# Two-layer cross-attention on one core: two row copies placed apart, a doubled result written by one add, and one projection step put later

## The chip, the cores and the metric

The kernel runs on one core of a Trainium2 chip. The metric is the time of one execution in microseconds of device time. Engines are named as in the profile: PE (TensorE, its weight loads apart as PEld), DVE (VectorE), ACT (ScalarE), POOL (GpSimd) and SP (SyncE, which issues most DMAs).

## The reference

Two attention layers follow each other on 16 images of 256 tokens with 320 channels, against a context of 256 rows with 512 channels. The first 77 context rows are text in layer 1 and the others image tokens; in layer 2 the last four are image tokens. The first layer, cut to what matters here:

```
text, ip = ctx[:, :77], ctx[:, 77:]
text_out = softmax(q_h @ k_h.T * scale) @ v_h              # 20 heads of 16
scores   = q_h @ ip_k_h.T * scale                          # per head
sem      = softmax(q @ k_text.T * scale) @ text @ ip.T * scale   # all heads alike
ip_probs = softmax(scores + 0.5 * sem) * spatial_mask
out      = (text_out + ip_probs @ ip_v_h) @ Wout + bout + x
```

Layer 2 has the same frame, with a semantic term of its own for each head (normalised rows of the text average against normalised image rows) that is added to the scores of the four image tokens.

## The kernel before

**Tiling.** The 20 heads of an image are worked in NG = 5 groups of four. One group of one image is a *slot*: 80 slots of layer 1 (`slot0(k)`, image k // 5, group k % 5), then 80 of layer 2 (`slot1(k)`). Beside a slot's own work run *tasks*: generators for the projections of keys, queries and values, the semantic term and the output projection (`close0`, `close1`), each with a list of due times counted in slots. `fill(now)` steps all tasks that are due, by the smallest due time.

**Layer 1.** For each group a stacked query tile Q (`qs`) and key tile K (`ks`) are built. Their first 77 rows carry the semantic term: the transposed text probabilities `tph`, copied to all four heads of Q (the T copy, L621, 77x1024), and the semantic key rows M, copied into the image columns of K (the M copy, L623, 77x716). Both are ACT's. Below these rows come the group's own rows, loaded by two DMAs ("K" and "Q"). Four such stacks exist; for the first four groups of an image the rows must be copied, and with LEAD = 4 it was done for group k + 4 at the end of slot k. `score0` multiplies K and Q (PE L650) and DVE takes the maxima of text and image columns (L651, L652). `maxima0` turns them on PE (L658), casts them on ACT (mt, L660) and puts them into Q by a DMA from ACT's queue (L661). `turned0` multiplies with keys on the rows (PE L673), takes exponentials on ACT (L676) and multiplies them by the semantic exponentials on POOL (L679), for two halves t of the keys. `attend0` multiplies by the values (PE L709). `settle0` transposes (DVE L720), divides (L723 to L726) and adds the text and the image part into `hsn` on POOL (L727). `hsn` has room for six groups; the fifth is written twice, by the add and then by a copy (L729).

**Output projection.** `close0` and `close1` go through `finish`: for three pairs of groups a 128x256 piece is made in a PSUM bank (in layer 1 by a DVE transpose of `hsn`, L953), and split into a rounded and a remainder part (ACT L744, DVE L746; for the third pair DVE L748). Then `project` multiplies by the output weights in three steps (PE L523, tile names `ho` and `wF`), and DVE adds bias and residual (L763).

**Layer 2.** `maxima1` (PE L801), `attend1` (PE L836, L838), `both1` (PE L784, L789) and `norm1` (PE L823, DVE L826, L828) play the same parts; L491 is the last of the DVE instructions that build the tile `gm` of the next image from an X bank.

**What sets the order.** Only PE's order is the program's own. For ACT, DVE, POOL and SP a scheduler orders the instructions. `queued(inst, *behind)` puts an instruction behind others of its engine without a wait: behind those named, or behind the last one marked by `anchor` on that engine (in layer 1 the DVE maxima L652, the exponentials and the POOL multiplies). PSUM is parted into three X banks, in which all projections, transposes and semantic products take turns, two T banks, one P bank and one of two banks' size for the scores.

Of the kernel before, what the change touches and what calls it, by code (L numbers as in the profile page):

```python
# [16 lines left out]
B = 16  # L17
S = 256
# [5 lines left out]
T0 = 77  # L24
# [13 lines left out]
NS = B * NG  # L38
LEAD = 4


def RAMP(t):
    return t if t < -5 or t > 3 else (t + 5) * 0.375
# [5 lines left out]
def xattn2(  # L49
# [27 lines left out]
    nc = tc.nc  # L77
    f = lambda ap: ap.bitcast(F32)
    mm = nc.tensor.matmul

    def dma(out, in_):
        nc.sync.dma_start(*(f(ap) if ap.dtype == FR else ap for ap in (out, in_)))  # L82
# [6 lines left out]
    def bank(tag="X"):  # L89
        return ps.tile([128, 512], F32, tag=tag, name=tag, bufs=BANKS[tag])  # L90
# [449 lines left out]
    def stack_rows(d):  # L540
        return d.rearrange("r (d h) t -> (r d) h t", h=HP)
# [64 lines left out]

    QK, P, W, R = {}, {}, {}, {}

    def stacks0(k, parts="KQTM"):
        b, g = divmod(k, NG)  # L610
        Q, K = QK[k] = qs[k % SIZES["NR"]], ks[k % SIZES["NR"]]
        hs = slice(4 * g, 4 * g + 4)
        for part in parts:
            if part == "K":
                dma(K[T0 : T0 + XROW], stack_rows(kd[0][b // 2][:, :, b % 2])[:, hs])
            elif part == "Q":
                dma(Q[T0 : T0 + XROW], stack_rows(get("q0", b)[1])[:, hs])
            elif g < SIZES["NR"]:
                tph, mh = get("s0", b)[1::2] if part == "T" else (None, get("m0t", b))
                if part == "T":  # L620
                    nc.scalar.copy(Q[:T0], f(tph[:, 0:1]).to_broadcast([T0, 4, S]))  # L621
                else:
                    nc.scalar.copy(K[:T0, :, T0:], f(mh[:, 0:1, T0:]).to_broadcast([T0, 4, S - T0]))  # L623


    def stacks1(k):
        b, g = divmod(k - NS, NG)
        n = 2 * SIZES["NR"]
        i = ((NS - SIZES["NR"]) % SIZES["NR"]) * 2 + (k - NS) % n
        Q, K = QK[k] = [x[i // 2 % SIZES["NR"]][:, 2 * (i % 2) : 2 * (i % 2) + 2] for x in (qs, ks)]  # L630
        get("k1", b)
        qd = get("o1", b)[0]
        for u in range(2):
            rows = slice(64 * u, 64 * u + XROW)
            hs = slice(4 * g + u, 4 * g + u + 3, 2)
            if k - NS < n:
                dma(K[64 * u + XROW : 64 * u + KS1], w1["ind"])
            dma(K[rows], stack_rows(kd[1][b][:, :, 0])[:, hs])
            dma(Q[rows], stack_rows(qd)[:, hs])
# [14 lines left out]
    def maxima0(k, queue=nc.scalar):  # L654
        Q, mn = QK[k][0], maxes[k]
        mp = bank()
        for t in range(2):
            mm(mp[:8, t * 128 : (t + 1) * 128], mn[:, t].rearrange("p a h -> p (a h)"), ident_r, start=True, stop=True)  # L658
        mt = buf("mt", [8, S], FR)
        nc.scalar.copy(mt, mp[:8, :S])  # L660
        issues[k] = queue.dma_start(f(Q[KS0 - 2 : KS0]), f(mt))  # L661

    def turned0(k, t):
# [17 lines left out]
    def attend0(k):  # L681
        b, g = divmod(k, NG)
        v, pv = get("v0", b), bank("P")
        for vt in range(3):
            values0(k, pv, v, vt)
        settle0(b, g, pv)

    def slot0(k):
        if k > 0:
            yield lambda: maxima(k + 1)  # L690
        yield lambda: ahead(k + 2, 0)
        yield lambda: turned0(k, 0)
        yield 0.2
        if k == 2:
            yield lambda: stacks(k + LEAD - 1)
        if k > 0:
            yield lambda: attend0(k - 1)
        yield lambda: ahead(k + 2, 1)
        yield lambda: turned0(k, 1)
        if k != 1:  # L700
            yield lambda: stacks(k + LEAD)
        yield 0.6
        yield 1.0

# [12 lines left out]
    def settle0(b, g, pv):  # L717
        hn = hsn
        nt = buf("nt", [128, 2, 8, 32], bufs=2)
        nc.vector.transpose(nt.rearrange("p a f c -> p (a f c)"), pv)  # L720

        rz = pv[:, :16].rearrange("p (a f) -> p a f", a=2)
        nc.vector.reciprocal(rz, nt[:, :, :, 16])  # L723
        nc.vector.tensor_mul(rz[:, 1], rz[:, 1], mk)
        tmp = buf("tmp", [128, 2, 8, 16], bufs=2)
        nc.vector.tensor_mul(tmp, nt[:, :, :, 0:16], rz.unsqueeze(3).to_broadcast([128, 2, 8, 16]))  # L726
        nc.gpsimd.tensor_add(hn[:, g // 2, :, g % 2], tmp[:, 0], tmp[:, 1])  # L727
        if g == NG - 1:
            nc.gpsimd.tensor_copy(hn[:, 2, :, 1], hn[:, 2, :, 0])  # L729

    def gather(b):

# [207 lines left out]
    def close1(b):  # L940
        hT, (pT, bd) = results["gathered", b], get("i1", b)

        def rows(p, hp):
            mm(hp, bd[:, p * 128 : (p + 1) * 128], pT, start=True, stop=True)  # L944
            nc.vector.tensor_add(hp, hT[:, p], hp)

        y = yield from finish(1, b, load(x1d[b], "xc"), rows)
        dma(out_d[b].rearrange("(k p) t -> p k t", p=128), y)

    def close0(b):  # L950

        def rows(p, hp):
            nc.vector.transpose(hp, hsn[:, p].rearrange("p f r d -> p (f r d)"))  # L953

        x1 = yield from finish(0, b, resid0.pop() if b == 0 else load(xT_d[b], "xc"), rows)
        dma(x1d[b].rearrange("(k p) t -> p k t", p=128), x1)
# [21 lines left out]
    def task(key, times, make, *needs):  # L978
        tasks[key] = [times, 0, make, needs, len(tasks)]
# [14 lines left out]
    def get(*key):  # L994
        while key not in results:
            step(key)
        return results[key]
# [20 lines left out]
    def shifted(n, *times):  # L1018

        return [RAMP(n + t) for t in times]  # L1020
# [10 lines left out]
    for c in range(B // 2):  # L1031
        n, k = 10 * c, [("k0", c)] if c else []
        task(("k0", c), FIRST["k0"] if c == 1 else shifted(n, -14.4, -13.3, -13, -12.4, -12, -10.8, -10.4, -9.8, -9.4, -8.8, -8.4), (lambda c=c: keys0(c)) if c else first_keys,
             *([("w4", 0)] if c > 1 else []))
        task(("q0", 2 * c), shifted(n, -11.8, -11, -10, -9, -8), lambda b=2 * c: queries0(b))
        task(("q0", 2 * c + 1), shifted(n, -4.4, -4, -3, -2.8, -2), lambda b=2 * c + 1: queries0(b))
        task(("m0t", 2 * c), shifted(n, -7.4), lambda b=2 * c: tokens0(b), *k)
        task(("m0t", 2 * c + 1), shifted(n, -4.8), lambda b=2 * c + 1: tokens0(b), *k)
        task(("v0", 2 * c), shifted(n, -7, -5.4, -5), lambda b=2 * c: values0_(b), *k)
        task(("v0", 2 * c + 1), shifted(n, -4, -3.8, -3.4), lambda b=2 * c + 1: values0_(b), *k)  # L1040
        for b, t in ((2 * c, (-7.4, -6.4, -6, -5.4, -5, -4.4, -3.4)), (2 * c + 1, (-2.4, -1.4, -1, -0.8, -0.4, 0, 1.2))):
            task(("s0", b), FIRST["s0"] if b == 1 else shifted(n, *t), lambda b=b: semantic0(b), ("q0", b), ("m0t", b))
            task(("c0", b), shifted(5 * b, *((5.6, 6, 6.2, 7.2, 7.6, 8.2) if b % 2 == 0 else (5.6, 6, 6.2, 7.2, 8.2, 9.2) if b < B - 1 else (6.33, 6.67, 7, 7.67, 8, 8.67))), lambda b=b: close0(b), ("w4", 0))
    for b in range(B):
        n = NS + 5 * b
        task(("k1", b), shifted(n, -7, -6.67, -6.33, -5.67, -5, -4.67), lambda b=b: keys1(b), ("w2",), *([("t1", b - 1)] if b else []), *([("w4", 1)] if b > 2 else []))
        task(("t1", b), shifted(n, -3.67, -3, -2.67, -2.33), lambda b=b: tokens1(b), ("k1", b), ("w3", b % 2))
        task(("o1", b), shifted(n, -7.67, -7, -6.67, -5.33, -4.33, -4), lambda b=b: open1(b), ("w7",), ("c0", b), *([("o1", b - 1)] if b else []))
        task(("i1", b), shifted(n, 6.67, 6.67, 6.67, 6.67, 7.33, 7.33, 7.67, 7.67, 8, 8.33), lambda b=b: image_softmax(b, NG - 1 if b == B - 1 else 0), ("gathered", b), ("taken", B + b - 1), *([("i1a",)] if b == B - 1 else []))
        task(("c1", b), shifted(n + (1.67 if b > B - 3 else 0), 8.67, 9, 9.33, 10, 11.67, 13), lambda b=b: close1(b), ("i1", b), ("w4", 1))  # L1050
    task(("i1a",), [2 * NS + 0.1], lambda: image_softmax(B - 1, 0, NG - 1), ("i1", B - 2))
    spread = lambda t, d, n: [t + d * i for i in range(n)]
    thirds = lambda n, t: [t + i // 3 + (0.2, 0.6, 1.0)[i % 3] for i in range(n)]
# [6 lines left out]
    task(("w4", 0), [2.6, 2.8, 3, 3.2], lambda: weights4(0), ("k0", 1))  # L1060
    task(("w4", 1), spread(NS + 4, 0.33, 4), lambda: weights4(1), ("c0", B - 1))

    def stacks(k):
        if 0 <= k < 2 * NS:
            (stacks0 if k < NS else stacks1)(k)

    def ahead(k, t):
        if k < NS:
            score0(k, t)
        else:  # L1070
            both1(k - 2, t)

    def maxima(k):
        if k < 2 * NS:
            (maxima0 if k < NS else maxima1)(k)
# [131 lines left out]
```

## Time and profile before

| | us |
|---|---|
| three runs | 1600.88, 1594.26, 1597.96 (median 1597.96) |
| the profiled execution: its own time | 1597.92 |
| its span in the trace | 1596.1 |
| mean granted TensorE clock | 0.983 |
| a pair of images in layer 1, from one of the waits at L650 to the next (126.50, 208.72, 290.94 us) | 82.22 |
| an image in layer 2, from one wait at L523 to the next (867.77, 921.31 us) | 53.54 |

A row of a group gives line, engine, operation, tiles and shapes, then its busy time, the mean of one in ns, and the idle time of the engine ahead of it with what ended it. A row of the timeline gives start, length, engine and instruction (several in a row of one kind as xN), and in brackets the idle time ahead of it and its releaser. Layer 1 runs to about 700 us, layer 2 behind it.

### The profile page before, as it was taken

Reading aid. Unit: us, or ns where it says so; the run is one execution under the profiler, and the core shown is the slowest. Engines: PE = TensorE matmul, PEld = TensorE weight load, DVE = VectorE, ACT = ScalarE, POOL = GpSimd, SP = SyncE. Lnnn points to the kernel's source line nnn. Section 1 sums busy time; section 2 is a strip of 40 time slices with the busy share of each in tenths; the row PEclk is TensorE's granted clock in tenths of the full one; section 3 lists DMA queues with packets and bytes.
Section 4 is the critical chain, followed back from the end, with each engine's and each line's share of the span. In section 5 each row is a group of like instructions: output and inputs, shape, how many; then the busy total and the mean of one; then the engine's idle time right before and its main releaser. Section 6 shows DMA issues by size and latency. Waiting matters only on the chain.

```text
span 1596.1 us, 35022 instructions
## 1 busy us (share of the span) xinstructions
PE 1493.3 (94%) x12666; PEld 1213.0 (76%) x12666; DVE 1211.1 (76%) x2468; ACT 944.8 (59%) x2071; POOL 1162.0 (73%) x1194
## 2 busy tenths in 40 slices
PE   7798989898989999799999999999999999999997
PEld 6677878787878888577777777777777777777765
DVE  5366667676767687887888888888888888888796
ACT  5556666666666676655565555555555555555563
POOL 3458787877777777787777777777777777767775
PEclk9999999999999999899999999999999999999999
DMA  6755556564646374555424333433344243423301
GB/s 217 183 151 158 156 153 169 143 173 119 187 124 189 113 208 117 151 180 176 130 85 130 122 121 97 137 122 112 106 128 131 87 131 112 144 82 106 111 26 55
DMA packets 206425, 213.09 MB, mean 134 GB/s; under 512 B 29162, under 2 KB 190156, under 8 KB 206252
## 3 DMA queue, kind: packets, MB, share of 16 engines
q1 hardware_dynamic: 204512, 209.56, 44.9%
q8 instruction: 100, 1.64, 0.4%
q10 hardware_dynamic: 1740, 1.30, 0.3%
q14 instruction: 73, 0.60, 0.1%
HBM read 121.21 MB, written 88.18 MB: 131 GB/s over the span
## 4 chain that ended last, share of the span: by engine, by line
PE 80%; DVE 6%; ACT 4%; POOL 4%; issue 3%; DMA 2%; SPq 1%; ACTq 0%; POOLq 0%; DVEq 0%
PE X L205 20%; PE X L823 16%; PE X L523 11%; PE P L709 6%; PE S L650 5%; PE P L836 4%; PE T L673 4%; PE T L784 4%; PE P L838 3%; PE S L789 2%; POOL P L679 2%; PE X L572 1%; PE X L944 1%; DVE mn L790 1%; SPq L82 1%
## 5 line engine op out<-in xcount | busy, mean ns | idle before, releaser
L679 POOL TENSOR_TENSOR P<-P,rs 128x512 f32<-128x512 f32 x320 | 410.1, 1303 | 140.3 <-ACT P L676 139.4
L814 POOL TENSOR_TENSOR wt<-P,ctb 128x512 f32<-128x512 f32 x320 | 417.1, 1320 | 117.0 <-ACT ctb L813 116.6
L823 PE MATMUL X<-ctb,gm 128*128 128x512 f32 x1120 | 330.1, 413 | 2.0 <-DVE wt L826 1.8
L676 ACT ACTIVATE P<-T 128x512 f32<-128x512 f32 x320 | 174.7, 593 | 147.8 <-PE T L673 137.7
L795 ACT ACTIVATE P<-T 128x512 f32<-128x512 f32 x320 | 174.0, 597 | 127.1 <-PE T L784 126.3
L813 ACT ACTIVATE ctb<-P 128x512 fp32r<-128x512 f32 x320 | 195.2, 632 | 60.8 <-PE X L823 59.8
L823 PEld LDWEIGHTS X<-ctb,gm 128*128 128x128 f32 x1120 | 189.5, 188 | 48.6 <-DVE wt L826 2.8
L790 DVE TENSOR_REDUCE mn<-S 128x4 fp32r<-128x1008 f32 x160 | 192.0, 1200 | 0.2 <-PE S L789 0.2
L826 DVE TENSOR_TENSOR wt<-X,wt 128x512 f32<-128x512 f32 x240 | 161.8, 679 | 10.7 <-PE X L823 9.7
L652 DVE TENSOR_REDUCE mn<-S 128x4 fp32r<-128x716 f32 x160 | 142.6, 891 | 0.0
L650 PE MATMUL S<-ks,qs 125*128 125x256 f32 x640 | 117.2, 307 | 18.2 <-DVE ho L748 17.2
L523 PE MATMUL X<-ho,wF 128*128 128x256 f32 x768 | 111.1, 288 | 22.7 <-DVE gm L491 18.7
L709 PE MATMUL P<-P,vr 128*32 128x256 f32 x1920 | 124.1, 390 | 4.1 <-DVE tmp L726 1.8
L650 PEld LDWEIGHTS S<-ks,qs 125*128 125x128 f32 x640 | 88.5, 194 | 51.3 <-issue 30.0
L523 PEld LDWEIGHTS X<-ho,wF 128*128 128x128 f32 x768 | 100.3, 191 | 28.8 <-issue 21.3
L205 PE MATMUL X<-cta,wA 128*128 128x252 f32 (+1 forms) x720 | 100.9, 286 | 17.4 <-ACT mt L660 8.3
L523 PE MATMUL X<-hq,wE 128*128 128x256 f32 x768 | 110.8, 288 | 5.8 <-ACT hq L512 3.0
L651 DVE TENSOR_REDUCE mn<-S 128x4 fp32r<-128x308 f32 x160 | 75.0, 468 | 50.2 <-PE S L650 50.1
L523 PEld LDWEIGHTS X<-hq,wE 128*128 128x128 f32 x768 | 104.5, 195 | 10.8 <-ACT hq L512 3.5
L205 PEld LDWEIGHTS X<-cta,wA 128*128 128x128 f32 x720 | 92.8, 192 | 21.9 <-ACT mt L660 9.6
L673 PE MATMUL T<-qs,ks 127*128 127x256 f32 x640 | 106.4, 289 | 2.0 <-DVE tph L594 1.3
L828 POOL TENSOR_TENSOR wt<-wt 128x512 f32<-128x512 f32 x80 | 103.6, 1295 | 4.7 <-DVE wt L826 4.7
(203 smaller groups left out, 2992.0 us busy)
## 6 DMA issues: line engine op xcount, KB each, us to landing
qd<-q SPq DMA_DIRECT2D x96, 384.0 KB
kd<-kst SPq DMA_DIRECT2D x73, 256.0 KB
rawc<-in_cT_dram SPq DMA_DIRECT2D x60, 256.0 KB
qs<-qd SPq DMA_DIRECT2D x80, 192.0 KB
ks<-kd SPq DMA_DIRECT2D x80, 192.0 KB
ks<-kd SPq DMA_DIRECT2D x160, 96.0 KB
qs<-qd SPq DMA_DIRECT2D x160, 96.0 KB
kd<-kst SPq DMA_DIRECT2D x21, 512.0 KB
```

The lines of the kernel that those rows point to most:

```text
L205: last = mm(out, lhs(a, k), rhs(b, k), start=i == 0, stop=i == len(terms) - 1)
L523: mm(pp, w(s, k, slice(m * 128, (m + 1) * 128)), a[:, t], start=i == 0, stop=i == len(terms) - 1)
L650: mm(sp[:, h], Q[: XROW + T0, h, t * 128 : (t + 1) * 128], K[: XROW + T0, h], start=True, stop=True)
L673: mm(st[p][:, j], K[:KS0, 2 * p + j, t * 128 : (t + 1) * 128], Q[:KS0, 2 * p + j], start=True, stop=True)
L676: exp = anchor(nc.scalar.activation(pt, st[p], AF.Exp, scale=SCALE))
L679: anchor(nc.gpsimd.tensor_mul(pt, pt, rs[:, t : t + 1].to_broadcast([128, 2, S])))
L709: mm(pv[32 * s : 32 * s + 32, o : o + S], v[:, vt, h : h + 32], P[k, s // 2][:, t, s % 2], start=vt < 2, stop=vt != 1,)
L790: anchor(nc.vector.tensor_reduce(maxes[k + 2][:, t], sp[:, :, :T1], axis=AX.X, op=ALU.max))
L795: anchor(nc.scalar.activation(P[k, u][:, t], st[u], AF.Exp, scale=SCALE))
L813: nc.scalar.activation(R[k, u][:, t], P[k, u][:, t], AF.Copy, scale=0.5)
L814: anchor(nc.gpsimd.tensor_sub(W[k, u][:, t], P[k, u][:, t], f(R[k, u][:, t])))
L823: mm(yp, gm[:, gb], R[k, u][:, kt], start=i == 0, stop=i == len(blocks[n]) - 1)
```

## The change

It has four parts.

1. The two copies of semantic rows are issued apart, and one slot earlier in their own group's terms: group k + 3 in slot k in place of group k + 4 at its end. The M copy is issued right after `maxima0`, queued behind the newest cast mt. The T copy is issued after `attend0`, ahead of the second half of `turned0`, queued behind the exponentials of the first half. The DMAs of K and Q stay at the end of the slot, for group k + 4. As the T copy alone asks for the whole semantic task, the end of that task is no longer forced at the end of a slot.
2. For the last group, one POOL add of 128x256 with its operands broadcast writes both places of `hsn`; the copy goes. Layer 2's copy (L890) stays.
3. The third step of `close0` (the transpose of the last pair of groups) is due at 6.6 and not at 6.2 slots of its image.
4. The last step of `close1` (the third projection step of layer 2) is due at 13.33 and not at 13.

```diff
+    casts = []
+
     def stacks0(k, parts="KQTM"):
...
-                tph, mh = get("s0", b)[1::2] if part == "T" else (None, get("m0t", b))
+                order = queued if k > 3 else lambda inst, *behind: inst
                 if part == "T":
-                    nc.scalar.copy(Q[:T0], f(tph[:, 0:1]).to_broadcast([T0, 4, S]))
+                    order(nc.scalar.copy(Q[:T0], f(get("s0", b)[1][:, 0:1]).to_broadcast([T0, 4, S])))
                 else:
-                    nc.scalar.copy(K[:T0, :, T0:], f(mh[:, 0:1, T0:]).to_broadcast([T0, 4, S - T0]))
+                    m = f(get("m0t", b)[:, 0:1, T0:]).to_broadcast([T0, 4, S - T0])
+                    order(nc.scalar.copy(K[:T0, :, T0:], m), *casts[-1:])
...
-        nc.scalar.copy(mt, mp[:8, :S])
+        casts.append(nc.scalar.copy(mt, mp[:8, :S]))
...
     def slot0(k):
         if k > 0:
             yield lambda: maxima(k + 1)
+            yield lambda: stacks(k + LEAD - 1, "M")
         yield lambda: ahead(k + 2, 0)
         yield lambda: turned0(k, 0)
         yield 0.2
         if k == 2:
-            yield lambda: stacks(k + LEAD - 1)
+            yield lambda: stacks(k + LEAD - 1, "KQ")
         if k > 0:
             yield lambda: attend0(k - 1)
+            yield lambda: stacks(k + LEAD - 1, "T")
         yield lambda: ahead(k + 2, 1)
         yield lambda: turned0(k, 1)
         if k != 1:
-            yield lambda: stacks(k + LEAD)
+            yield lambda: stacks(k + LEAD, "KQ")
...
-        nc.gpsimd.tensor_add(hn[:, g // 2, :, g % 2], tmp[:, 0], tmp[:, 1])
         if g == NG - 1:
-            nc.gpsimd.tensor_copy(hn[:, 2, :, 1], hn[:, 2, :, 0])
+            a, b = [tmp[:, t].unsqueeze(2).to_broadcast([128, 8, 2, 16]) for t in range(2)]
+            nc.gpsimd.tensor_add(hn[:, 2], a, b)
+        else:
+            nc.gpsimd.tensor_add(hn[:, g // 2, :, g % 2], tmp[:, 0], tmp[:, 1])
...
-            task(("c0", b), shifted(5 * b, *((5.6, 6, 6.2, 7.2, 7.6, 8.2) if b % 2 == 0 else (5.6, 6, 6.2, 7.2, 8.2, 9.2) if b < B - 1 else (6.33, 6.67, 7, 7.67, 8, 8.67))), lambda b=b: close0(b), ("w4", 0))
+            task(("c0", b), shifted(5 * b, *((5.6, 6, 6.6, 7.2, 7.6, 8.2) if b % 2 == 0 else (5.6, 6, 6.6, 7.2, 8.2, 9.2) if b < B - 1 else (6.33, 6.67, 7, 7.67, 8, 8.67))), lambda b=b: close0(b), ("w4", 0))
...
-        task(("c1", b), shifted(n + (1.67 if b > B - 3 else 0), 8.67, 9, 9.33, 10, 11.67, 13), lambda b=b: close1(b), ("i1", b), ("w4", 1))
+        task(("c1", b), shifted(n + (1.67 if b > B - 3 else 0), 8.67, 9, 9.33, 10, 11.67, 13.33), lambda b=b: close1(b), ("i1", b), ("w4", 1))
```

Lines of the changed file stand three to eight lower than those of before (L650 is L653, L660 is L663, L676 is L679, L679 is L682, L709 is L714, L748 is L755; the T copy is L623, the M copy L626, the add of the last group L734).

What the change does to the order is seen at three places. The first is where an even image of layer 1 ends. POOL, before (`hq` is a query split, `M` the semantic keys):

```order
L513 TENSOR_TENSOR hq_275<-xq_120,hq_275 128x512
L727 TENSOR_TENSOR hsn<-tmp_776 128x8x16
L679 TENSOR_TENSOR P_94<-P_94,rs_467 128x512
L679 TENSOR_TENSOR P_91<-P_91,rs_467 128x512
L729 COPY hsn<-hsn 128x8x16
L353 MEMSET M_318 77x2x77
```

and with the change:

```order
L513 TENSOR_TENSOR hq_275<-xq_120,hq_275 128x512
L734 TENSOR_TENSOR hsn<-tmp_776 128x256
L682 TENSOR_TENSOR P_94<-P_94,rs_467 128x512
L682 TENSOR_TENSOR P_91<-P_91,rs_467 128x512
L682 TENSOR_TENSOR P_94<-P_94,rs_467 128x512
```

The last heads are complete after the one add, ahead of the multiplies and no longer behind two of them. PE at the same place, before (the `wD` products are value projections of the next pair of images):

```order
L709 MATMUL P<-P_93,vr 32x256 x2
L650 MATMUL S<-ks_177,qs_173 128x256 x4
L673 MATMUL T<-qs_175,ks_179 128x256 x4
L600 MATMUL X<-tph_424,M_318 128x256
L601 MATMUL X<-tph_424,M_318 128x256
L600 MATMUL X<-tph_424,M_318 128x256
L601 MATMUL X<-tph_424,M_318 128x256
L205 MATMUL X<-wD,cta_79 128x320 x3
L205 MATMUL X<-wD,cta_80 128x320 x3
```

and with the change:

```order
L714 MATMUL P<-P_93,vr 32x256 x2
L653 MATMUL S<-ks_177,qs_173 128x256 x4
L676 MATMUL T<-qs_175,ks_179 128x256 x4
L205 MATMUL X<-wD,cta_79 128x320 x3
L205 MATMUL X<-wD,cta_80 128x320 x3
L205 MATMUL X<-wD,ctb_81 128x320 x3
L205 MATMUL X<-wD,ctb_82 128x320 x3
L600 MATMUL X<-tph_424,M_318 128x256
L601 MATMUL X<-tph_424,M_318 128x256
```

The semantic products now stand behind twelve value products. The second place is one slot of layer 1 on ACT. Before:

```order
L676 ACTIVATE P_92<-T 128x512
L676 ACTIVATE P_93<-T 128x512
L621 CAST qs_176<-tph_424 77x1024
L623 CAST ks_180<-M_318 77x4x179
L147 CAST kst_223<-X 128x2x179
L593 CAST tph_425<-X 77x256
L531 CAST q_280<-X 128x256
L660 CAST mt_183<-X 8x256
L661 DMA qs_174<-mt_183 2x4x256
L676 ACTIVATE P_94<-T 128x512
L676 ACTIVATE P_91<-T 128x512
L744 CAST ho_225<-X 128x256
```

and with the change:

```order
L679 ACTIVATE P_93<-T 128x512
L147 CAST kst_223<-X 128x2x179
L593 CAST tph_425<-X 77x256
L531 CAST q_280<-X 128x256
L663 CAST mt_183<-X 8x256
L626 CAST ks_180<-M_318 77x4x179
L664 DMA qs_174<-mt_183 2x4x256
L679 ACTIVATE P_94<-T 128x512
L679 ACTIVATE P_91<-T 128x512
L623 CAST qs_176<-tph_424 77x1024
L751 CAST ho_225<-X 128x256
```

The M copy has moved behind the cast mt, ahead of that cast's DMA and the next exponentials; the T copy behind those exponentials. The third place is in layer 2, on PE. Before:

```order
L801 MATMUL X<-ident_r,mn_531 4x128 x2
L523 MATMUL X<-ho_225,wF_983 128x256 x8
L836 MATMUL P<-P_94,v1t 32x256
L836 MATMUL P<-P_91,v1t 32x256
...
L838 MATMUL P<-wt,zone 32x256 x4
L784 MATMUL T<-qs_176,ks_180 128x256 x4
```

and with the change (the six repeats of L836 and L843 left out):

```order
L808 MATMUL X<-ident_r,mn_531 4x128 x2
L843 MATMUL P<-P_94,v1t 32x256
L843 MATMUL P<-P_91,v1t 32x256
...
L845 MATMUL P<-wt,zone 32x256 x4
L791 MATMUL T<-qs_176,ks_180 128x256 x4
L796 MATMUL S<-ks_177,qs_173 128x256 x4
L830 MATMUL X<-ctb_81,gm 128x512 x4
L523 MATMUL X<-ho_225,wF_981 128x256 x8
```

The projection step moves from ahead of the value products to behind them, the next scores and four products of the semantic norm.

More of the change, by code (lines that the diff above doesn't have):

```diff
@@ L1061, in xattn2, with stacks @@
     task(("w4", 1), spread(NS + 4, 0.33, 4), lambda: weights4(1), ("c0", B - 1))
-    def stacks(k):
-        if 0 <= k < 2 * NS:
-            (stacks0 if k < NS else stacks1)(k)
+    def stacks(k, parts="KQ"):
+        if 0 <= k < NS:
+            stacks0(k, parts)
+        elif k < 2 * NS and "K" in parts:
+            stacks1(k)
     def ahead(k, t):
```

## The prediction

> **What bounds the kernel now.** I read the page first: engine totals, then the chain that ended last, then the waits, and only then single places on the timeline.
>
> ```profile
> PE 1493.3 (94%) x12666; PEld 1213.0 (76%) x12666; DVE 1211.1 (76%) x2468; ACT 944.8 (59%) x2071; POOL 1162.0 (73%) x1194
> PE 80%; DVE 6%; ACT 4%; POOL 4%; issue 3%; DMA 2%; SPq 1%; ACTq 0%; POOLq 0%; DVEq 0%
> ```
>
> PE is busy for 1493.3 of 1596.1 us, so about 103 us of PE idle is all that a reordering can win, besides time in which PE is busy at a lower clock. No other engine is above 76%. The list of waits on PE says where that idle time sits, as total, times and longest:
>
> ```profile
> PE X L523 <- DVE gm L491: 18.7, 13, 1.4
> PE S L650 <- DVE ho L748: 17.2, 6, 2.9
> PE X L205 <- ACT mt L660: 8.3, 6, 1.4
> PE X L591 <- ACT sp L587: 5.1, 1, 5.1
> PE X L523 <- ACT mt L660: 3.3, 5, 0.7
> PE P L838 <- DVE wt L828: 3.0, 7, 0.8
> PE P L709 <- POOL P L679: 1.5, 2, 0.9
> ```
>
> The change touches the first five. I call the second A, the third B, the fifth C (all once per pair of images in layer 1) and the first D (once per image in layer 2). The start and the end of the span are not touched.
>
> **Wait A (last group's heads, third transpose later).** One occurrence, by engine:
>
> ```profile
> 204.11 0.45 POOL L727 TENSOR_TENSOR hsn<-tmp 128x128 f32<-128x128 f32 x1
> 204.53 2.49 POOL L679 TENSOR_TENSOR P<-P,rs 128x512 f32<-128x512 f32 x2
> 206.97 0.28 POOL L729 COPY hsn<-hsn 128x128 f32<-128x128 f32 x1
> 207.29 0.46 DVE L953 STREAM_TRANSPOSE X<-hsn 128x256 f32<-128x256 f32 x1 [3.62 <-POOL hsn L729]
> 208.19 0.48 DVE L748 SCALAR_TENSOR_TENSOR ho<-ho,tmask,X 128x256 fp32r<-128x256 f32 x1 [0.44 <-ACT ho L744]
> 204.35 1.50 PE L709 MATMUL P<-P,vr 128*32 128x256 f32 x24
> 208.72 0.94 PE L650 MATMUL S<-ks,qs 125*128 125x256 f32 x4 [2.87 <-DVE ho L748]
> ```
>
> POOL puts two multiplies (2.49 us) between the add L727 and the copy L729 that completes the last heads. The transpose, ACT's cast of it (L744), the correction L748 and PE follow in single file. L650 writes S and needs no ho; L748 frees an X bank, and the matmul that wants one is L600, two rows below. In the new order one add stands where L727 stood and nothing comes between it and the transpose: it can start at 204.11. No 128x256 add is in the trace. Below it is the 128x128 add, above it the 128x512 multiply:
>
> ```profile
> L727 POOL TENSOR_TENSOR hsn<-tmp 128x128 f32<-128x128 f32 x80 | 38.7, 484 | 5.9 <-DVE tmp L726 5.9
> L679 POOL TENSOR_TENSOR P<-P,rs 128x512 f32<-128x512 f32 x320 | 410.1, 1303 | 140.3 <-ACT P L676 139.4
> ```
>
> So 484 to 1303 ns; on the line between them 256 elements give 484 + 819/3 = 757 ns, which I take, as the size lies nearer to 128. It replaces 484 + 280 = 764 ns, so POOL's load is unchanged (at 1303 it would be 8.5 us more over 16 images, in POOL's 434 us of idle time). The transpose then starts near 204.9, and the chain of 1.38 us (207.29 to 208.67) ends near 206.3, or 206.8 with the dear add. PE ends L709 at 205.85. It then has L650 and L673, and the new order puts the twelve wD products ahead of L600, so ho is ready some two us before it is asked for. The wait goes whole: **17.2 us**.
>
> Behind each A the granted clock halves. The rows of the table by windows give the window and its length, busy time and count for PE, PEld, DVE, ACT and POOL, then the granted clock (1.00 is full), the DMA share and GB/s; two rows of the timeline stand below:
>
> ```profile
> 127.20:130.50 3.30, 3.30 (x16) 3.30 (x15) 2.05 (x5) 2.77 (x5) 1.95 (x3) 0.50 0.42 108
> 205.70:209.10 3.40, 0.53 (x7) 0.38 (x4) 1.38 (x3) 0.80 (x2) 1.55 (x3) 1.00 0.29 102
> 209.10:212.50 3.40, 3.40 (x17) 3.40 (x16) 2.25 (x6) 2.31 (x4) 1.49 (x3) 0.50 0.28 78
> 373.00:379.60 6.60, 6.42 (x27) 6.42 (x28) 2.80 (x7) 4.51 (x9) 3.85 (x5) 0.50 0.25 60
> 540.20:543.50 3.30, 3.30 (x15) 3.30 (x15) 1.71 (x5) 3.30 (x6) 2.71 (x4) 0.50 0.40 119
> 229.00:232.40 3.40, 2.01 (x19) 1.67 (x21) 3.23 (x9) 2.83 (x8) 3.40 (x4) 1.00 1.04 232
> ...
> 209.46 1.05 PE L673 MATMUL T<-qs,ks 127*128 127x256 f32 x4
> 215.12 0.64 PE L673 MATMUL T<-qs,ks 127*128 127x256 f32 x4
> ```
>
> Six such stretches follow the six waits, five of about 3.4 us and one of twice that. The same four matmuls take 1.05 us in one and 0.64 outside, so a stretch of 3.4 us loses 3.4 x (1 - 0.64/1.05) = 1.33 us (at most half, 1.7). Seven times 1.33 is **9.3 us** (at most 11.9, at least nothing). The last window row shows a wait of 1.39 us (B) that leaves the clock at 1.00. [...]
>
> **Waits B and C (copies of semantic rows).** ACT now does both copies after the second exponentials and ahead of the cast mt, for which PE waits:
>
> ```profile
> 226.72 1.09 ACT L676 ACTIVATE P<-T 128x512 f32<-128x512 f32 x2 [1.37 <-PE T L673]
> 230.28 0.36 ACT L660 CAST mt<-X 8x256 fp32r<-8x256 f32 x1
> 230.69 0.92 PE L205 MATMUL X<-cta,wA 128*128 128x192 f32 x6 [1.39 <-ACT mt L660]
> ...
> 184.22 1.09 ACT L676 ACTIVATE P<-T 128x512 f32<-128x512 f32 x2 [2.17 <-PE T L673]
> 186.28 0.52 PE L673 MATMUL T<-qs,ks 127*128 127x256 f32 x3
> 187.45 1.21 PE L523 MATMUL X<-ho,wF 128*128 128x256 f32 x8 [0.66 <-ACT mt L660]
> ```
>
> The copies, by the group rows below 1.04 and 0.79 us long, stand between the two and hold mt up by 1.83 us, more than either wait, so B (8.3 us) and C (3.3 us) both vanish: **11.6 us**. The copies are not removed:
>
> ```profile
> L621 ACT CAST qs<-tph 77x1024 fp32r<-77x1024 f32 x64 | 66.6, 1042 | 0.0
> L623 ACT CAST ks<-M 77x716 fp32r<-77x716 f32 x64 | 50.7, 793 | 0.0
> L676 ACT ACTIVATE P<-T 128x512 f32<-128x512 f32 x320 | 174.7, 593 | 147.8 <-PE T L673 137.7 <-POOL hsn L727 2.8 <-ACT mt L660 1.5
> ```
>
> ACT waits 137.7 us for T ahead of exponentials, and the moved copies ask for 117.3 us of that. The T copy goes ahead of the second half's exponentials, into the 1.37 and 2.17 us of the rows above: hidden. Behind it are only those exponentials, and POOL's multiplies and PE's L709 behind them. The M copy goes behind mt and ahead of the first half's exponentials. Those wait for L673, which ends at 186.80; PE had mt at 187.45, so without the pair ahead of it mt can be there from 185.6 and the M copy done at 186.4. It is hidden, with little to spare; uncovered it would cost 0.79 us. The DMA of mt, issued from ACT's queue behind mt, may go out up to 0.8 us later, and its rows are read a slot (8 us) later. The K and Q loads keep their place on SP. One group less of lead for the copies leaves about a slot between copy and score matmul. For what I can't see (other casts of ACT, DVE's second row transposes, which now stand behind a reciprocal) I take off half a microsecond per pair, **-3 us**, with bounds of 0 and -12 (B and C returning under another name).
>
> **Wait D (third projection step of layer 2).**
>
> ```profile
> 1080.45 0.28 PE L801 MATMUL X<-ident_r,mn 128*4 128x128 f32 x2
> 1082.17 1.18 PE L523 MATMUL X<-ho,wF 128*128 128x256 f32 x8 [1.45 <-DVE gm L491]
> 1083.29 1.07 PE L836 MATMUL P<-P,v1t 128*32 128x256 f32 x16
> 1084.17 0.61 PE L838 MATMUL P<-wt,zone 128*32 128x256 f32 x8
> 1081.94 0.68 DVE L828 TENSOR_TENSOR wt<-wt,X 128x512 f32<-128x512 f32 x1
> ```
>
> L523 waits for an X bank until L491 has read it. With the step later, L836 can start at 1080.73 and takes 0.88 us to the start of L838, so L838 is up at 1081.61. But the odd heads of L838 need wt of DVE's L828, which is queued behind L491 and ends at 1082.62; DVE's order here doesn't change. A wait of about 1.0 us for L828 takes the place of the 1.45 us for L491 (the list of waits has that wait seven times already). The gain is 0.45 us, 13 times: **6 us**. Its ends are 0 and the full 18.7.
>
> **Layer 1's tail.** The wait of 5.1 us at L591 comes once, with ACT late for L587; the new order has those activations ahead of the second exponentials, but weight casts move up as well. I take **+3 us**, between -2 and +5.
>
> **The sum.** 17.2 + 9.3 + 11.6 - 3 + 6 + 3 = 44.1 us. The profiled execution took 1597.92 us (span 1596.1), and the median of the three runs is 1597.96, so the base is the same: 1597.9 - 44.1 = **1554 us**, 2.8% faster.
>
> **Rivals.**
> - *POOL takes over in layer 1.* With A, the clock, B and C gone, a pair of images shrinks by some 6 us. Where POOL works without a gap the wait would return as L709 for L679, which today costs 1.5 us. B and C are then not won: 1566. For it speaks the window at 229, with POOL busy in all of its 3.40 us; against it POOL's 27% of idle time.
> [...]
> - *L838 finds wt ready.* If L826 and L828 move up with the matmuls ahead of them, D is won whole: 1554 - 12.7 = 1541.
> - *The change doesn't do what it says at A.* If the add is late because tmp is (POOL waited 5.9 us for it in all), A and its clock stay: 1580.
> - *The T copy holds up the exponentials (slower).* Where ACT has less than 1.04 us of idle ahead of the second half, the copy delays exponentials, multiplies and L709 in a slot. If that held in all 64 slots without slack behind, 66.6 us would be lost: 1554 + 67 = 1621; it passes no change at two thirds of the slots. Against it: the mean idle per wait is 137.7/121 = 1.14 us, and PE has hardly waited for L679.
>
> **How the numbers follow.** Forecast 0.55 (1546 to 1562); POOL 0.14; clock 0.07; L838 ready 0.08; A stays 0.05; the T copy 0.11, half of it past no change. The range 1538 to 1578 leaves out the last two and the end of the third. A measurement of this kernel can tell about 0.5% (8 us) from no change: faster 0.88, same 0.06, slower 0.06.
>
> **What would show it.** A right: no wait of L650's successor on ho, POOL's new add near 0.76 us, and no granted clock of 0.5 in layer 1 after 120 us but near its end. B and C right: no wait of PE on mt, and the two copies at the old durations in what was idle. D right: PE waits for L828 at the L838 matmuls, about 1.0 us, 13 times, and no longer for L491. Wrong: a wait of PE for L679 or for exponentials of more than 10 us in all, or score matmuls that wait for a copy.

## The result and the profile after

| | before | changed |
|---|---|---|
| median, us | 1599.42 (4 runs, 1594.26 to 1601.93) | 1546.18 (4 runs, 1545.33 to 1548.67) |
| span of the profiled execution, us | 1596.1 | 1543.5 |
| mean granted TensorE clock | 0.983 | 0.992 |

The ratio is 0.9674, with a 95% interval of 0.9646 to 0.9702: 3.3% faster, where 2.8% (1554 us) was forecast.

The page's engine totals and its chain that ended last, of the changed kernel:

```profile
PE 1484.2 (96%) x12666; PEld 1202.0 (78%) x12666; DVE 1198.2 (78%) x2468; ACT 949.2 (61%) x2071; POOL 1165.0 (75%) x1178
PE 85%; DVE 6%; DMA 3%; POOL 2%; issue 2%; ACT 2%; SPq 0%; ACTq 0%; POOLq 0%; DVEq 0%
```

PE's work is the same number of instructions; its busy time falls by 9.1 us (the mean granted clock is 0.992 and was 0.983), the rest of the gain is idle time. The waits of PE, the costliest first (total, times, longest):

```profile
PE P L845 <- DVE wt L835: 11.1, 21, 0.9
PE X L661 <- DVE mn L655: 6.2, 7, 1.4
PE X L205 <- ACT wA L147: 6.1, 3, 5.1
PE S L653 <- DVE mn L655: 4.2, 5, 2.1
...
PE X L591 <- ACT sp L587: 2.2, 1, 2.2
```

The waits for ho (A), for mt (B and C) and for L491 (D) are gone. What took D's place heads the list, at less than its price (11.1 us against 18.7; 3.0 us of it were there before). The table by windows (window, length, busy time and count of PE, PEld, DVE, ACT, POOL, then granted clock, DMA share, GB/s) shows five pairs of images:

```profile
105.00:524.00 419.00, 417.23 (x3985) 364.27 (x3984) 299.58 (x723) 303.09 (x655) 354.01 (x322) 1.00 0.61 166
```

PE is busy for 417.23 of 419.00 us, at full clock. By this row under 2 us of listed idle time are left there for an order to win; whether PE could do the same work in less busy time, the row doesn't say.

To see where the 52.6 us between the two spans come from, take the start of the same matmul in both traces, here the product that turns the maxima (L658, then L661; in layer 2 L801, then L808):

| place | before, us | changed, us | ahead by |
|---|---|---|---|
| layer 1, group 20 | 228.02 | 216.26 | 11.8 |
| group 30, one pair of images on | 310.25 | 291.86 | 18.4 |
| group 40 (a pair with a slow stretch twice as long) | 393.89 | 367.42 | 26.5 |
| group 60 | 558.40 | 518.55 | 39.9 |
| layer 2, first | 724.21 | 680.32 | 43.9 |
| layer 2, group 75 | 1521.62 | 1468.13 | 53.5 |

A pair of images takes 75.60 us instead of 82.23.

### The profile page after: what moved, and what is told of

It reads as the page before. It is cut to its first block, busy times and chain, and to the rows that moved or that the text cites. A ratio compares the mean times of both kernels' runs of the same rounds, so it can differ in the third digit from the quotient of the medians.

```text
span 1543.5 us, 35120 instructions
## 1 busy us (share of the span) xinstructions
PE 1484.2 (96%) x12666; PEld 1202.0 (78%) x12666; DVE 1198.2 (78%) x2468; ACT 949.2 (61%) x2071; POOL 1165.0 (75%) x1178
## 4 chain that ended last, share of the span: by engine, by line
PE 85%; DVE 6%; DMA 3%; POOL 2%; issue 2%; ACT 2%; SPq 0%; ACTq 0%; POOLq 0%; DVEq 0%
PE X L205 23%; PE X L830 17%; PE X L523 11%; PE P L714 7%; PE S L653 6%; PE T L676 4%; PE T L791 4%; PE P L843 4%; PE P L845 3%; PE S L796 2%; PE X L951 1%; PE X L572 1%; DVE wt L835 1%; POOL P L682 1%; PE X L661 1%
## 5 line engine op out<-in xcount | busy, mean ns | idle before, releaser
L682 POOL TENSOR_TENSOR P<-P,rs 128x512 f32<-128x512 f32 x320 | 413.5, 1316 | 116.6 <-ACT P L679 116.6
L679 ACT ACTIVATE P<-T 128x512 f32<-128x512 f32 x320 | 174.8, 593 | 97.6 <-PE T L676 73.5
L833 DVE TENSOR_TENSOR wt<-X,wt 128x512 f32<-128x512 f32 x240 | 161.8, 679 | 11.1 <-PE X L830 10.9
L714 PE MATMUL P<-P,vr 128*32 128x256 f32 x1920 | 124.6, 389 | 2.5 <-POOL P L682 1.2
L653 PE MATMUL S<-ks,qs 125*128 125x256 f32 x640 | 114.8, 302 | 4.2 <-DVE mn L655 4.2
L523 PE MATMUL X<-hq,wE 128*128 128x256 f32 x768 | 110.3, 287 | 6.8 <-ACT hq L512 4.0
L653 PEld LDWEIGHTS S<-ks,qs 125*128 125x128 f32 x640 | 86.5, 190 | 36.9 <-issue 30.4
L523 PEld LDWEIGHTS X<-hq,wE 128*128 128x128 f32 x768 | 102.8, 194 | 10.8 <-ACT hq L512 4.5
L523 PE MATMUL X<-ho,wF 128*128 128x256 f32 x768 | 108.8, 285 | 0.7 <-DVE ho L753 0.6
L676 PE MATMUL T<-qs,ks 127*128 127x256 f32 x640 | 104.7, 286 | 0.0
L523 PEld LDWEIGHTS X<-ho,wF 128*128 128x128 f32 x768 | 100.8, 190 | 4.6 <-DVE ho L753 1.1
L791 PEld LDWEIGHTS T<-qs,ks 50*128 50x128 f32 x640 | 47.7, 184 | 61.7 <-issue 33.2
```

The costliest lines, as they stand in the source:

```text
L523: mm(pp, w(s, k, slice(m * 128, (m + 1) * 128)), a[:, t], start=i == 0, stop=i == len(terms) - 1)
L653: mm(sp[:, h], Q[: XROW + T0, h, t * 128 : (t + 1) * 128], K[: XROW + T0, h], start=True, stop=True)
L676: mm(st[p][:, j], K[:KS0, 2 * p + j, t * 128 : (t + 1) * 128], Q[:KS0, 2 * p + j], start=True, stop=True)
L679: exp = anchor(nc.scalar.activation(pt, st[p], AF.Exp, scale=SCALE))
L682: anchor(nc.gpsimd.tensor_mul(pt, pt, rs[:, t : t + 1].to_broadcast([128, 2, S])))
L714: mm(pv[32 * s : 32 * s + 32, o : o + S], v[:, vt, h : h + 32], P[k, s // 2][:, t, s % 2], start=vt < 2, stop=vt != 1,)
```

## The experiments

Each is timed against the kernel before, in three rounds; its ratio stands beside the changed kernel's 0.9674. The edits are against the changed kernel or the one before, as said.

**Part 1 alone.** The other parts are taken out of the changed kernel.

```diff
-            a, b = [tmp[:, t].unsqueeze(2).to_broadcast([128, 8, 2, 16]) for t in range(2)]
-            nc.gpsimd.tensor_add(hn[:, 2], a, b)
+            nc.gpsimd.tensor_copy(hn[:, 2, :, 1], hn[:, 2, :, 0])
...
-(5.6, 6, 6.6, 7.2, 7.6, 8.2)
+(5.6, 6, 6.2, 7.2, 7.6, 8.2)
...
-8.67, 9, 9.33, 10, 11.67, 13.33)
+8.67, 9, 9.33, 10, 11.67, 13)
```

> Part 1 alone (the two copies apart; add, copy and both due times as before). Theory 1, redundant parts: the wait at the score matmul goes by this part alone, because the new order of the semantic products moves the place of the wait for ho from L650 to a projection that stands some 4 us later; gain 17 (wait) + 12 (clock) + 11.6 (mt) + 4 (tail of layer 1) = 45 us, so ratio 0.972, and POOL still has two multiplies between add and copy. Theory 2, the prediction's step: the add is what ends the wait, so with add and copy as before the wait of 2.87 us and the half clock stay six times, gain 12 to 16 us, ratio 0.991.

Measured: 1560.55 us, ratio 0.9767 (0.9751 to 0.9784). The wait is gone, but the expectation had POOL's order wrong. In the built program the copy now stands right behind the add. POOL and DVE on the timeline:

```profile
196.11 0.47 POOL L732 TENSOR_TENSOR hsn<-tmp 128x128 f32<-128x128 f32 x1
196.64 0.29 POOL L734 COPY hsn<-hsn 128x128 f32<-128x128 f32 x1
196.89 2.53 POOL L682 TENSOR_TENSOR P<-P,rs 128x512 f32<-128x512 f32 x2
...
197.86 0.48 DVE L753 SCALAR_TENSOR_TENSOR ho<-ho,tmask,X 128x256 fp32r<-128x256 f32 x1 [0.44 <-ACT ho L749]
...
196.10 1.15 PE L205 MATMUL X<-wD,cta 128*128 128x320 f32 x6 [1.10 <-ACT P L679]
...
199.49 0.74 PE L653 MATMUL S<-ks,qs 125*128 125x256 f32 x4
```

So ho is ready at 198.34, 1.15 us before the score matmul starts: moving the copies made the scheduler shorten this chain too. That is why the gain (37 us) holds A. The waits for mt (B and C) go with this part too, and D keeps its 18.7 us. It falls short of the 45 us expected by a new wait of 1.10 us at wD in four pairs, among others.

**Part 1 with the old PE order.** As the run before, and the semantic task is forced to its end where it was.

```diff
+        if "Q" in parts and g < SIZES["NR"]:
+            get("s0", b)
```

> As the run before, but the semantic task is forced to its end where it was, so PE's order in layer 1 is that of before. Theory 1 (the wait stands on an instruction that doesn't need the bank, and its place shifts with small changes): here it stands on the projection that takes the bank, 24 matmuls after L650, so the wait goes though POOL's and PE's orders are the old ones; ratio 0.972. Theory 2 (the semantic product next takes the bank, as the prediction had it): the wait stays, 2 to 3 us, six times; ratio 0.991.

Measured: 1559.3 us, 0.9765 (0.9748 to 0.9781), as the run before. The moved semantic products have no part in the gain. POOL again has the copy right behind the add, so this run, like the one before, doesn't tell the length of the chain from the place of the wait.

**Part 2 alone** (the one add).

> Part 2 alone (one 128x256 add for add and copy). Both theories: the add ends the chain 2.4 us sooner, so the wait at L650 goes or is under 0.4 us, the clock recovers, gain 27 to 29 us; mt's waits (8.3 and 3.3 us) and layer 2's (18.7 us) stay. Ratio 0.982. If the add is not what did it: no change.

Measured: 1577.77 us, 0.9888 (0.9861 to 0.9914), 18 us where 27 to 29 were expected. The wait at L650 is gone, and waits of about 0.5 us come in its place (PE on the timeline):

```profile
201.11 1.14 PE L205 MATMUL X<-wD,cta 128*128 128x320 f32 x6 [0.51 <-ACT P L676]
```

There are six of about 0.5 us, four of this kind and two at L650 for ho, so here the wait still stands on L650 and the shorter chain hides most of it. These waits and one slow stretch (at 305.92 us) account for some 4 us of what is missing; the rest is not explained.

**Part 3 alone** (third step of the layer-1 close at 6.6).

> Part 3 alone (third step of the layer-1 close due at 6.6, not 6.2). Theory 1: the transpose's bank is taken later and DVE has a value transpose and two reductions ahead of it, so no early wait for ho is left on L650 although add and copy are as before: gain 25 to 29 us, ratio 0.983. Theory 2 (the add is needed): the wait stays, within 0.5% of before.

Measured: 1573.03 us, 0.9857 (0.9835 to 0.9879), 23 us where 25 to 29 were expected. PE's order is that of before, and POOL keeps its two multiplies between add and copy. The timeline, POOL, DVE and PE:

```profile
199.84 0.45 POOL L727 TENSOR_TENSOR hsn<-tmp 128x128 f32<-128x128 f32 x1
200.25 2.52 POOL L679 TENSOR_TENSOR P<-P,rs 128x512 f32<-128x512 f32 x2
202.72 0.28 POOL L729 COPY hsn<-hsn 128x128 f32<-128x128 f32 x1
...
206.61 0.48 DVE L748 SCALAR_TENSOR_TENSOR ho<-ho,tmask,X 128x256 fp32r<-128x256 f32 x1 [2.04 <-ACT ho L744]
...
201.52 0.74 PE L650 MATMUL S<-ks,qs 125*128 125x256 f32 x4
202.09 0.65 PE L673 MATMUL T<-qs,ks 127*128 127x256 f32 x4
```

ho is ready at 207.09, 5.6 us after the score matmul started, and nothing waits for it. So L650 never needed ho.

**A longer chain.** With part 2 alone, the third piece's cast of even images is written four times more.

```diff
+            for _ in range(4 if l == 0 and p == 2 and b % 2 == 0 else 0):
+                nc.scalar.copy(hl[:, p], hp)
             split_from(hl, p, hp)
```

> Part 2 alone, and for even images of layer 1 the third piece's cast is written four times more by ACT (0.37 us each, the same value), so the chain to ho is some 1.5 us longer than in the run with part 2 alone. In the built program the wait for ho then stands on the projection that takes the bank and not on L650 or L673. Theory 1 (place of the wait decides): no wait at L650, and not slower than part 2 alone, ratio 0.983 to 0.989. Theory 2 (length of the chain decides): a wait of 1.5 to 2 us six times, with half clocks up to 19 us slower than part 2 alone, ratio 0.995 to 1.000.

Measured: 1580.15 us, 0.9886 (0.9864 to 0.9908), as part 2 alone. DVE and PE:

```profile
204.03 0.48 DVE L750 SCALAR_TENSOR_TENSOR ho<-ho,tmask,X 128x256 fp32r<-128x256 f32 x1 [2.06 <-ACT ho L746]
...
203.21 0.74 PE L650 MATMUL S<-ks,qs 125*128 125x256 f32 x4
```

ho is ready 1.30 us after the score matmul's start, without a wait. The reason stands in the built programs. Their PE rows at this place, with the semaphores that each waits for, before:

```
L650 MATMUL S<-ks_177,qs_173 128x256 [waits DVE_49]
...
L205 MATMUL X<-wD,ctb_82 128x320 x3
L523 MATMUL X<-hq_275,wE_84 128x256
L523 MATMUL X<-hq_275,wE_84 128x256 [waits Pool_49]
```

In the kernel before, the value that L650 waits for is the count that L748 (ho) brings; in this run it is that of the score reduction L652, two DVE instructions earlier, and the count of that instruction (there L750) is waited for by the first L523 of `hq`, 24 matmuls further on, which takes the bank. The traces show the semaphores at the same matmuls (L523 waits for one of DVE's in this run and for none before), but not the counts; these stand in the programs alone. Why the compiled program puts the wait early in one case and not in the other stays open.

**The changed kernel without part 2, and without part 3.**

> The changed kernel with part 2 undone (add and copy as before, POOL's two multiplies between them). Theory 1 (any one part removes the wait): the wait for ho stands on the semantic product, behind twelve value products; no wait at the score matmul; ratio 0.966 to 0.970, as the changed kernel. Theory 2 (the prediction's step, the add is what ends the wait): 17 us of waits and the half clocks come back, ratio 0.984.

> The changed kernel with part 3 undone. The wait for ho stands on the key product L676 right behind the scores, with the short chain of part 2: theory 1 gives up to 0.5 us six times and no half clocks, as in the run with part 2 alone, so at most 4 us over the changed kernel, ratio 0.967 to 0.970. If the third step is what ends the wait: 0.984.

Measured: 1546.82 us, 0.9684 (0.9668 to 0.9700), and 1543.96 us, 0.9670 (0.9653 to 0.9687). Neither can be told from the changed kernel. Without part 2 the copy stands right behind the add again. So either of parts 2 and 3 adds nothing measurable once the other is there. Parts 1 and 4 without both were not run; as part 1 alone is 38.3 us ahead of before at layer 2's first group and the changed kernel 43.9, the two may be worth some 5 us between them. The gains of the four parts alone (37, 18, 23 and 5 us by their ratios) sum to 83 us, and together they are 52, mainly since three of them remove the same wait.

**Part 4 alone** (layer 2's projection step).

> Part 4 alone (third projection step of layer 2 at 13.33). If the whole of layer 2's difference between the two profiles (9.6 us) is this part's: ratio 0.994, and PE waits for DVE's L828 at L838 13 times, about 0.54 us each, in place of 1.45 us for L491. The prediction's 0.45 us an image would give 6 us, ratio 0.996. If layer 2 gained for another reason: 1.000.

Measured: 1593.22 us, 0.9971 (0.9957 to 0.9984). The waits for L491 are gone, and those of L838 for L828 grow from 3.0 to 10.9 us. In its trace layer 2 gains 7.5 us from its first group to group 75, while that first group starts 0.9 us later than before, though PE's order in layer 1 is unchanged.

**Layer 2's closing products behind the next scores.** Against the changed kernel; `zones1` takes the products on wt and `settle1` over from `attend1`.

```diff
             yield lambda: attend1(k - 2)
         yield lambda: both1(k, 0)
+        if k > NS + 1:
+            yield lambda: zones1(k - 2)
```

> The changed kernel, with the closing products of layer 2's attention (8 matmuls on wt, all 80 slots) issued after the next scores and not ahead of them, so DVE's sum has about 0.75 us more. If the 13 waits of 0.54 us that are left (11.1 us in all slots) are worth what they show: 7 to 11 us below the changed kernel, ratio 0.961 to 0.963. If the wait moves on to the norm products or the later DVE work: same as the changed kernel, 0.967.

Measured: 1550.65 us, 0.9709 (0.9691 to 0.9728): 4 to 6 us slower than the changed kernel, though the two intervals still touch. The wait for wt goes and another comes, as often and about as long each time (waits of PE; L846 is its L843, L810 the cast mt):

```profile
PE P L846 <- ACT mt L810: 6.3, 13, 0.5
```

An image of layer 2 gets longer in the trace, 53.09 against 52.52 us on the mean of 15; neither expectation had that, and its cause is not shown. No version here is clearly faster than the changed kernel.

**Copies doubled.** The changed kernel with every T copy done twice, and in another run every M copy.

```diff
+                    for _ in range(2):
-                    order(nc.scalar.copy(Q[:T0], f(get("s0", b)[1][:, 0:1]).to_broadcast([T0, 4, S])))
+                        order(nc.scalar.copy(Q[:T0], f(get("s0", b)[1][:, 0:1]).to_broadcast([T0, 4, S])))
```

> The changed kernel with every T copy done twice (64 x 1.04 us more of ACT work, between the first half's exponentials and what follows). If the copies lie in ACT's idle time, as the prediction has it: under 8 us slower than the changed kernel, ratio up to 0.972. If T copies hold up the second half's exponentials (the rival): most of 67 us, ratio about 1.00.

> The changed kernel with every M copy done twice (64 x 0.79 us more of ACT work between mt and the first half's exponentials). The prediction has 0.4 us to spare there, so about 0.4 us of each is uncovered for ACT; if POOL and PE have slack behind it: under 8 us slower than the changed kernel, ratio up to 0.972. If the exponentials are on PE's path there: 64 x 0.4 = 25 us, ratio 0.983, up to 50 us with no slack, 0.998.

Measured: the T copies 1548.74 us, 0.9701 (0.9670 to 0.9732); the M copies 1558.53 us, 0.9763 (0.9747 to 0.9778). ACT's idle time ahead of the layer-1 exponentials shows where the 67 us of T copies went. The group row of the exponentials, changed kernel:

```profile
L679 ACT ACTIVATE P<-T 128x512 f32<-128x512 f32 x320 | 174.8, 593 | 97.6 <-PE T L676 73.5 <-POOL P L682 11.2 <-PE X L601 4.5
```

and with the T copies doubled:

```profile
L680 ACT ACTIVATE P<-T 128x512 f32<-128x512 f32 x320 | 174.4, 593 | 53.0 <-PE T L677 29.2 <-POOL P L683 11.6 <-PE X L601 4.5
```

45 us of it came out of that idle time (97.6 less 53.0); where the rest went is not shown. The M copies have less room: they cost 12 to 14 us, between the two expectations (under 8, or 25). One wait per pair appears on PE (timeline),

```profile
195.51 1.11 PE L205 MATMUL X<-wC,cta 128*128 128x320 f32 x6 [1.50 <-DVE P L730]
```

and in its trace a pair takes 1.4 us longer (76.96 against 75.57); in the other slots no wait of this kind shows. Up to group 60 that makes 8.8 us, and 5.2 more are lost between there and layer 2, where a single wait of 5.5 us stands at the products with the values (its L715).

## Why the prediction was right, point by point

| term | forecast, us | from the traces, us | how |
|---|---|---|---|
| A | 17.2 | 17.6 | 6 x 2.94: from the start of L709's row to L650 4.37 us (204.35, 208.72), in part 2 alone 1.43 (203.06, 204.49) |
| half clock | 9.3 | 9.9 | 7 x 1.41, the pair with the long stretch (83.64) less the others (82.23) |
| B, C | 11.6 | 13.4 | 6 x 1.55 + 5 x 0.81 |
| unseen new waits | -3 | 0 | none in the window of five pairs |
| layer 2 | 6 | 9.6 | 53.5 - 43.9 |
| tail of layer 1 | 3 | 4.0 | 43.9 - 39.9; holds the sixth B (1.55) |
| sum | 44.1 | 53.0 (54.5 less the B told twice) | the spans differ by 52.6 |

**A.** Right in size and in what makes ho early. The new add takes 740 ns by the median of its 16 (757 were taken). In the changed kernel:

```profile
196.46 0.75 POOL L734 TENSOR_TENSOR hsn<-tmp 128x256 f32<-128x256 f32 x1
197.16 2.54 POOL L682 TENSOR_TENSOR P<-P,rs 128x512 f32<-128x512 f32 x2
...
198.14 0.48 DVE L755 SCALAR_TENSOR_TENSOR ho<-ho,tmask,X 128x256 fp32r<-128x256 f32 x1 [0.44 <-ACT ho L751]
...
198.47 0.74 PE L653 MATMUL S<-ks,qs 125*128 125x256 f32 x4
```

Here too the score matmul starts 0.15 us before ho is ready (198.62), so the wait no longer stands on it. Two statements of that step were wrong. In the order of before, the bank that L748 frees was not wanted by L600: the `hq` projection, 24 matmuls on, waits for it in the run with the longer chain, whose PE order is that of before; on L650 the wait merely stood (part 3 alone shows the same). And the add was not needed: with the copies moved, POOL's copy follows its add at once (part 1 alone; the changed kernel without part 2). The prediction credited the wait's end to the one add and to the products moved ahead of L600; each of parts 1, 2 and 3 ends it alone (part 2 but for two waits of 0.45 us), and the moved products have no share in it (part 1 gains the same with the old PE order). The sum came out because it counted the wait once, whatever ended it.

**The clock.** With the six waits gone, the slow stretches behind them go: the granted clock is 1.00 from 105 to 524 us, as the window row shows. So slow stretches without these waits, to which the forecast gives 0.07 (clock), did not come about there. Behind the first longer wait afterwards, of 2.07 us, one is back, in the changed kernel's PE rows and the window behind them:

```profile
524.97 0.74 PE L653 MATMUL S<-ks,qs 125*128 125x256 f32 x4 [2.07 <-DVE mn L655]
...
526.00:529.00 3.00, 3.00 (x13) 3.00 (x12) 2.90 (x11) 1.77 (x6) 2.72 (x3) 0.50 0.67 193
```

How long a wait must be is not settled by this. In part 1 alone a wait of the same 2.07 us (L653 at 530.52) was followed by full clock. The waits of 1.39 us (B), which left the clock at full in the kernel before, were followed by half clock once with part 2 alone and once in the run with the longer chain (from 225.87 us). PE with part 2 alone, and the two windows from before the wait to behind it:

```profile
304.31 0.91 PE L205 MATMUL X<-cta,wA 128*128 128x192 f32 x6 [1.39 <-ACT mt L660]
...
302.51:305.92 3.41, 2.02 (x20) 1.72 (x22) 3.34 (x9) 2.84 (x8) 3.41 (x4) 1.00 1.03 232
305.92:309.33 3.41, 3.41 (x28) 1.77 (x29) 1.35 (x4) 1.35 (x7) 3.24 (x3) 0.50 1.05 322
```

With the T copies doubled, a stretch of half clock even starts at 562.70 us where PE is listed as busy for all of the 3.41 us ahead of it. So a wait of 2.87 us was followed by half clock six times in six, shorter ones (2.07 and 1.39 us) sometimes, and the listed length of one wait alone doesn't tell.

**B and C.** Right, and a little larger than listed. The wait before B, seen from the last matmul ahead of it:

```profile
228.78 0.52 PE L673 MATMUL T<-qs,ks 127*128 127x256 f32 x3
230.69 0.36 PE L205 MATMUL X<-cta,wA 128*128 128x192 f32 x1 [1.39 <-ACT mt L660]
```

Three matmuls of 0.28 us in 0.52 us start 0.12 us apart, so the last starts at 229.02 and, at that spacing, the next could start at 229.14. It starts at 230.69: 1.55 us lost, of which the list shows 1.39, because it counts from the modelled end of the last matmul. That, not another mechanism, makes the term 1.8 us short. In their own group's terms the copies come later by the change, not earlier: for group j in slot j - 3, where it was the end of slot j - 4. No score matmul waits for one all the same. The copies are hidden, the T copy amply; the M copy has the "little to spare" that the prediction gave it (both by the doubled copies).

**New waits.** The -3 us for what could not be seen was too cautious: the list of PE's waits has none between 105 and 524 us. (Parts 1 and 2 alone do bring such waits, of 1.1 and 0.5 us.)

**D.** Right in mechanism. The changed kernel's PE and DVE:

```profile
926.55 0.28 PE L808 MATMUL X<-ident_r,mn 128*4 128x128 f32 x2
926.76 1.07 PE L843 MATMUL P<-P,v1t 128*32 128x256 f32 x16
927.65 0.59 PE L845 MATMUL P<-wt,zone 128*32 128x256 f32 x2
928.78 0.63 PE L845 MATMUL P<-wt,zone 128*32 128x256 f32 x6 [0.54 <-DVE wt L835]
929.35 0.50 PE L791 MATMUL T<-qs,ks 50*128 50x256 f32 x4
...
928.05 0.68 DVE L835 TENSOR_TENSOR wt<-wt,X 128x512 f32<-128x512 f32 x1
```

The first head goes, the next waits for DVE's sum. From the maxima product to the next scores it is 2.80 us now and 4.27 before; the projection step costs 0.96 us later on, so 0.51 us an image are won (0.45 forecast), 13 times 6.6 us. The list says 0.54 and not 1.0 us for the new wait because the first two products, started 1.13 us before the others, are shown as busy for 0.59 of it. Layer 2 gained 7.5 us with part 4 alone and 9.6 us in the changed kernel; the 1 to 3 us above 6.6 are not explained.

**The rivals.** POOL did not take over: PE has no lasting wait for the multiplies. L838 did not find wt ready. The T copy does not hold up the exponentials: 67 us more of it cost 3 to 4 us, not clear of the uncertainty.

## What to carry to other kernels

A wait's place in the list names the instruction that carries it, which need not be the one that needs it: before paying for a shorter chain, see whether the waiting instruction uses the result at all, and if not, an edit elsewhere that shifts the order may end the wait, as parts 1 and 3 did. Parts of a change that remove the same wait are not to be summed; run each alone, and the whole without each. On PE a listed wait was a lower bound here (1.39 us listed for 1.55 lost), since it starts at the modelled end of a matmul that the next would have overlapped (0.28 us long, started 0.12 us apart).

## What the runs showed of the hardware

A wait of PE of 2.87 us was followed by a stretch of half granted clock six times in six; one of 2.07 us was so in the changed kernel and not in part 1 alone, and those of 1.39 us once in six with part 2 alone and not once in six in the kernel before. A stretch of 3.4 us costs 1.41 us here (a pair of images of 83.64 us against 82.23). A POOL add of 128x256 whose operands are broadcast in a middle dimension takes 0.74 us, close to the 0.757 on the line between a 128x128 add (0.48 us) and a 128x512 multiply (1.30 us).
